# Expert gate's logits with the gate's weights stationary, in four column tiles, and a transposition back

## Chip, cores and metric

The kernel runs on one core of a Trainium2 chip. The metric is the device time of one execution in microseconds; of the kernel before, three timed runs are shown, and one more execution was profiled. Engines: PE is TensorE (PEld its weight loads), DVE VectorE, ACT ScalarE, POOL GpSimd, SP SyncE, which issues most transfers.

## What is computed

One transformer block in float32 over 8 batches of 512 tokens with 256 features: attention with 16 heads and a decayed outer-product memory, a layer norm, a mixture of 8 experts (and two null experts) of which each token takes two, and a second layer norm. Cut to what matters here:

```python
x = _layernorm(x + attention(x))
gate_logits = x @ gate_w.T + gate_b            # 4096 x 256 by 256 x 10
gate_probs = softmax(gate_logits)
weights, selected = top_k(gate_probs, 2)       # null experts get weight 0, the rest is renormalised
combine_w = ...                                # 4096 x 8
out = einsum('te,teh->th', combine_w, einsum('td,edh->teh', x, expert_w) + expert_b)
x = _layernorm(x + out)
```

The change concerns the second line, the gate's logits.

## The kernel before

**Attention turns.** The frame of the program is a loop over 32 units (a batch and a group of four heads), each of eight turns. A turn issues, in this order: `products` (line 182), which computes score blocks twice, once for the running maximum (`mx`, line 192) and once for the exponentials (`sc`, line 196); in some turns projections of later units (`pq` line 165, `pv` line 175), the turned maxima (`pt`, line 233) or the values product (`po`, line 248); then `fill` (line 813), which adds other work. `mx` and `sc` have one PSUM buffer each. So the next turn's `mx` can start when VectorE has taken the maxima of the last (L206, L214) and ScalarE its copy of the diagonal (L210); GpSimd masks that copy (L211) and VectorE reduces it a turn later (L217). In the last turn of a unit the mask is added on TensorE (L205) and VectorE reduces the whole block (L206). A turn is named below by its `mx` block: `mx_2_1`, `mx_1_0`, `mx_1_1` (the last of a unit's cycle), `mx_0_0`.

**Planner.** All other work is written as generators which `fill` and `filled` advance while the program is built. Each turn adds a credit, from what TensorE is thought to have free. A generator yields what its step costs (`yield 0.9`), or `STEP` (go on in the next turn), or `POOL` (GpSimd is wanted, once a turn), or a condition. Generators in `chains` go first, then those in `bulk` (expert tiles, memory sums) as long as credit is left. What stays free in a turn is filled by warming matmuls (`idle`, line 811) that compute nothing that is used. So a step's stated cost decides which expert tile lands in which turn, and the order of every engine's instructions follows from it; this order is kept as written (`in_this_order`). Each engine works through its own list in order.

**The chain of one batch.** `prepare` (line 584) loads x (L596) and adds the output bias to it on GpSimd (L599), later the memory's share (L604, L605) and the inverted denominators (`recs`, L610, L616). `front` (line 636) does the output projection (`pa`), the first norm, eight transpositions of the normed tokens (`px`, L668; copied by ScalarE to `x1T`, L669), the gate's logits (`pg`, L674) and the chain of small VectorE operations on 128 partitions x 40 elements that takes the two best experts: `lg` (L683, adds the gate's bias), maximum, exponent, twice the choice of the largest (L696 to L709), then the weights (L712 to L728). `all_experts` (line 732) turns the weights (`pc`, L740: four matmuls of 32 columns each side by side, copied by ScalarE to `cT`), computes expert tiles (`pex`, L749), adds them with the token's weight on VectorE (L753), adds the bias (`pbias`, L761), and norms (L622 to L628) and stores (`out_y`, L770).

**The gate.** For each of four tiles of 128 tokens the tile of `x1T` is the stationary operand and the gate's weights `gws` (256 x 10, two halves of 128 rows) are the moving one: eight matmuls a batch, in the trace 16 passes, because each float32 matmul shows as two. The logits come out with the tokens on the partitions, 10 columns for each tile, and VectorE reads them from PSUM.

**The end.** The denominators of a batch's softmax go from the last `po` through DRAM: ScalarE's copy (`raw`, L257), store `den` (L258), load `rec` (L267), reciprocal on VectorE (L269), store `dr` (L271), two loads `recs`, GpSimd's product (L616), then `pa`. All these transfers, the loads of x and the stores `out_y` are issued by SP, in its order. PSUM banks other than those of `mx`, `sc` and `po` come from a ring of three (`bank`, line 87).

The lines of the kernel that the diff touches follow.

Of the kernel before, what the change touches and what calls it, by code (L numbers as in the profile page):

```python
# [10 lines left out]
F32 = mybir.dt.float32  # L11
BF16 = mybir.dt.bfloat16
AF = mybir.ActivationFunctionType
ALU = mybir.AluOpType
AX = mybir.AxisListType

P = 128
B, T, D, H, DH = 8, 512, 256, 16, 16
NT = T // P
KC = D // P  # L20
NG = 4
NE, NTRUE = 10, 8
# [12 lines left out]
STEP, POOL = "goes on at the next turn", "needs GpSimd"  # L35
# [22 lines left out]
def bc(ap, axis, n):  # L58

    ap = ap.unsqueeze(axis)  # L60
    shape = list(ap.shape)
    shape[axis] = n
    return ap.to_broadcast(shape)
# [13 lines left out]
def block_kernel(ctx, tc, x, xT, wqk, bqk, wtok, wod, memv, memvb, row, gw, we, eb, out):  # L77
    nc = tc.nc
    PS = bass.MemoryType.PSUM
    const = ctx.enter_context(tc.tile_pool(name="const", bufs=1))  # L80
# [6 lines left out]
    def bank(name):  # L87
        return psB.tile([P, 512], F32, tag="bank", name=name)
# [5 lines left out]
    def load_xT(b):  # L94
        nc.sync.dma_start(xt[:, b], xT[b].rearrange("(k p) t -> p k t", p=P))
# [10 lines left out]
    def vec(n):  # L106
        return rows[:, ROW[n][0] : ROW[n][1]]
# [13 lines left out]
        nc.sync.dma_start(wq[:, :, w, 1], wq_v[:, :, w, 1])  # L121
    for b in range(1, B):
        load_xT(b)
    gws = const.tile([P, KC, NE], F32, name="gws")
    nc.sync.dma_start(gws, gw.rearrange("(k p) e -> p k e", p=P))

    ident = const.tile([P, P], F32, name="ident")
    make_identity(nc, ident)
# [490 lines left out]
    def root(mv, nm):  # L619

        rs = ffp[0].tile([P, NT], F32, tag="rs", name=f"rs_{nm}")
        nc.vector.tensor_scalar(rs, mv[:, :, 1], EPS, None, ALU.add)  # L622
        rr = ffp[0].tile([P, NT], F32, tag="rr", name=f"rr_{nm}")
        nc.gpsimd.tensor_tensor(rr, rs, half, ALU.pow)  # L624
        return rr

    def norm(out_t, in_t, mv, rr, c):
        nc.vector.tensor_scalar(out_t[:, c, :], in_t[:, c, :], mv[:, c, 0:1], rr[:, c : c + 1],  # L628
                                ALU.subtract, ALU.mult)

    def stats(mv, in_t, c, nm):
        bs = ffp[0].tile([P, 6], F32, tag="bs", name=f"bs_{nm}_{c}")
        nc.vector.bn_stats(bs, in_t[:, c, :])
        nc.vector.bn_aggr(mv[:, c, :], bs)

    def front(b):

        yield lambda: b in prepared
        ff, osb, xb = ffp[0], st[b]["osb"], st[b]["xb"]
        y = xb  # L640
        mv = ff.tile([P, NT, 2], F32, tag="mv", name=f"mv1_{b}")
        for c in range(NT):
            pa = bank(f"pa{b}_{c}")
            for k in range(KC):
                nc.tensor.matmul(pa[:, D:], xt[:, b, k, c * P : (c + 1) * P], wt[:, k, CM : CM + D],  # L645
                                 start=(k == 0), stop=(k == KC - 1))
            for k in range(KC):
                nc.tensor.matmul(pa[:, :D], osb[:, k, c * P : (c + 1) * P], wo[:, k, :],  # L648
                                 start=(k == 0), stop=(k == KC - 1))
            nc.vector.scalar_tensor_tensor(y[:, c, :], pa[:, D:], gated[:, c, b : b + 1], xb[:, c, :],  # L650
                                           ALU.mult, ALU.add)
            nc.vector.tensor_tensor(y[:, c, :], y[:, c, :], pa[:, :D], ALU.add)
            stats(mv, y, c, f"a{b}")
            yield 1.9
        yield STEP
        x1 = y
        rr = root(mv, f"a{b}")
        yield STEP
        yield STEP
        for c in range(NT):  # L660
            norm(x1, y, mv, rr, c)
        yield STEP
        yield lambda: b < left[0] + 2
        x1T = ff.tile([P, KC, T], F32, tag="x1T", name=f"x1T_{b}")
        for k in range(KC):
            pt = bank(f"px{b}_{k}")
            for c in range(NT):
                nc.tensor.transpose(pt[:, c * P : (c + 1) * P], x1[:, c, k * P : (k + 1) * P], ident)  # L668
            nc.scalar.copy(x1T[:, k, :], pt)  # L669
            yield 0.7  # L670
        pg = bank(f"pg{b}")
        for c in range(NT):
            for k in range(KC):
                nc.tensor.matmul(pg[:, c * NE : (c + 1) * NE], x1T[:, k, c * P : (c + 1) * P], gws[:, k, :],  # L674
                                 start=(k == 0), stop=(k == KC - 1))
            if c == 1:
                yield 0.9

        def small(n, *shape):
            return ff.tile([P, NT, *shape], F32, tag=n, name=f"{n}_{b}", bufs=1)  # L680

        lg = small("lg", NE)
        nc.vector.tensor_tensor(lg, pg[:, : NT * NE].rearrange("p (c e) -> p c e", e=NE), bc(vec("gb"), 1, NT), ALU.add)  # L683
        yield 0.9
        m1 = small("m1")
        nc.vector.tensor_reduce(m1, lg, AX.X, ALU.max)

        ex = small("ex", NE)
        nc.vector.tensor_tensor(ex, lg, bc(m1, 2, NE), ALU.subtract)
        nc.scalar.activation(ex, ex, AF.Exp)  # L690
        fb = bc(first, 1, NT)
        hot, top = [], m1
        for r in range(2):

            eq = small("eq", NE)
            nc.vector.tensor_tensor(eq, lg, bc(top, 2, NE), ALU.is_equal)  # L696
            nc.vector.tensor_tensor(eq, eq, fb, ALU.mult)
            cd = small(f"cd{r}")
            nc.vector.tensor_reduce(cd, eq, AX.X, ALU.max)
            oh = small(f"oh{r}", NE)  # L700
            nc.vector.tensor_tensor(oh, fb, bc(cd, 2, NE), ALU.is_equal)
            hot.append(oh)
            if r == 0:
                l2 = small("l2", NE)
                nc.vector.scalar_tensor_tensor(l2.rearrange("p c e -> p (c e)"), oh.rearrange("p c e -> p (c e)"), -3.0e38,
                                               lg.rearrange("p c e -> p (c e)"), ALU.mult, ALU.add)
                lg = l2
                top = small("m2")
                nc.vector.tensor_reduce(top, l2, AX.X, ALU.max)  # L709
            yield STEP  # L710
        es = small("es")
        nc.vector.tensor_reduce(es, ex, AX.X, ALU.add)  # L712
        nc.vector.reciprocal(es, es)
        nc.vector.tensor_tensor(ex, ex, bc(es, 2, NE), ALU.mult)
        exf = ex.rearrange("p c e -> p (c e)")
        nc.vector.scalar_tensor_tensor(exf, exf, TINY, exf, ALU.is_ge, ALU.mult)
        w = small("lg", NE)
        nc.vector.tensor_tensor(w, hot[0], hot[1], ALU.add)
        nc.vector.tensor_tensor(w, w, ex, ALU.mult)
        yield STEP  # L720
        dn = small("dn")
        nc.vector.tensor_reduce(dn, w[:, :, :NTRUE], AX.X, ALU.add)
        nc.vector.scalar_tensor_tensor(dn, dn, 0.0, dn, ALU.is_equal, ALU.add)
        nc.vector.reciprocal(dn, dn)
        cwf = ff.tile([P, NT * NTRUE + 32 - NTRUE], F32, tag="cw", name=f"cw_{b}")
        nc.vector.memset(cwf[:, NT * NTRUE :], 0.0)
        cw = cwf[:, : NT * NTRUE].rearrange("p (c e) -> p c e", e=NTRUE)
        nc.vector.tensor_tensor(cw, w[:, :, :NTRUE], bc(dn, 2, NTRUE), ALU.mult)  # L728
        st[b].update(x1=x1, x1T=x1T, cw=cw, cwf=cwf)
        ready.add(b)  # L730
# [45 lines left out]
    def fronts():  # L776
        for b in range(B):
            yield from front(b)
# [78 lines left out]
    for u in range(-1, U + 1):  # L857
        b, g = UNITS[u] if 0 <= u < U else (0 if u < 0 else B, -1)
# [96 lines left out]
```

## Time and profile before

| | us |
|---|---|
| median of 3 runs | 934.79 (931.99 to 935.59) |
| profiled execution, its own time | 936.77 |
| its span | 935.1 |
| mean granted TensorE clock | 0.975 |
| gate: TensorE matmuls L674 (128 passes) | 15.7 busy |
| gate: weight loads L674 (128) | 15.5 busy |
| `lg`, L683 (8) | 1.6 busy |

The span runs from the first to the last instruction; the profiled execution's own time has 1.67 us around it. Busy times of TensorE are modelled at their ends and overlap between neighbouring passes, so the time that a group takes from others is better read from the starts of what stands before and behind it. Attention ends at about 816 us; what follows is mostly expert tiles of batches 5, 6 and 7.

### The profile page before, as it was taken

Reading aid. Unit: us, or ns where it says so; the run is one execution under the profiler, and the core shown is the slowest. Engines: PE = TensorE matmul, PEld = TensorE weight load, DVE = VectorE, ACT = ScalarE, POOL = GpSimd, SP = SyncE. Lnnn points to the kernel's source line nnn. Section 1 sums busy time; section 2 is a strip of 40 time slices with the busy share of each in tenths; the row PEclk is TensorE's granted clock in tenths of the full one; section 3 lists DMA queues with packets and bytes.
Section 4 is the critical chain, followed back from the end, with each engine's and each line's share of the span. In section 5 each row is a group of like instructions: output and inputs, shape, how many; then the busy total and the mean of one; then the engine's idle time right before and its main releaser. Section 6 shows DMA issues by size and latency. Waiting matters only on the chain.

```text
span 935.1 us, 14524 instructions
## 1 busy us (share of the span) xinstructions
PE 868.9 (93%) x5254; PEld 423.1 (45%) x5254; DVE 629.8 (67%) x1449; ACT 344.3 (37%) x746; POOL 376.4 (40%) x682
## 2 busy tenths in 40 slices
PE   8899978798889999999899999999999999999996
PEld 5545544454355544344444344434443344354442
DVE  1344688986876868766778568656765677486765
ACT  4265634344334353444344444343344332200000
POOL 1177785426476645522524345224532352110000
PEclk9999999999899999999989999999999999999998
DMA  7300000000010100000100010001000010010000
GB/s 255 99 13 17 8 7 5 2 2 3 27 46 14 35 27 24 1 2 28 46 1 2 5 55 15 1 3 41 31 2 2 27 47 1 2 48 1 22 23 23
DMA packets 25512, 23.73 MB, mean 25 GB/s; under 512 B 8348, under 2 KB 21180, under 8 KB 25440
## 3 DMA queue, kind: packets, MB, share of 16 engines
q1 hardware_dynamic: 24336, 22.24, 7.5%
q8 instruction: 41, 0.67, 0.3%
q0 software_dynamic: 48, 0.16, 0.2%
q10 hardware_dynamic: 1056, 0.40, 0.2%
q14 instruction: 31, 0.25, 0.1%
HBM read 16.75 MB, written 4.73 MB: 23 GB/s over the span
## 4 chain that ended last, share of the span: by engine, by line
PE 64%; DVE 22%; DMA 4%; POOL 4%; issue 3%; ACT 2%; POOLq 0%; SPq 0%; DVEq 0%; ACTq 0%
PE pex L749 21%; PE mx L192 14%; PE po L248 6%; PE pq L165 5%; DVE negdia L206 3%; DVE x L753 3%; PE pl L349 3%; PE pv L175 2%; PE pa L645 2%; DVE negmax L214 2%; PE pa L648 2%; PE sc L196 2%; PE mx L205 2%; DVE pr L520 1%; DVE ou L518 1%
## 5 line engine op out<-in xcount | busy, mean ns | idle before, releaser
L192 PE MATMUL mx<-qk,qk 32*128 32x128 f32 (+3 forms) x1024 | 219.4, 487 | 39.2 <-DVE negdia L206 27.1
L749 PE MATMUL pex<-ws,x1T 128*128 128x512 f32 x512 | 245.3, 614 | 4.1 <-DVE x L753 3.7
L224 ACT ACTIVATE pe<-sc 128x1024 f32<-128x1024 f32 (+3 forms) x256 | 181.6, 709 | 134.8 <-PE sc L196 122.9
L196 PE MATMUL sc<-qk,qk 32*128 32x512 f32 (+3 forms) x1024 | 211.2, 485 | 1.7 <-ACT pe L224 1.0
L753 DVE SCALAR_TENSOR_TENSOR x<-pex,cw,x 128x256 f32<-128x256 f32 x256 | 123.6, 483 | 101.7 <-PE pex L749 96.5
L226 POOL TENSOR_SCALAR_AFFINE_SELECT pe<-pe 128x256 f32<-128x256 f32 x256 | 105.9, 413 | 165.6 <-ACT pe L224 162.1
L192 PEld LDWEIGHTS mx<-qk,qk 32*128 32x128 f32 x1024 | 84.9, 186 | 154.5 <-DVE negdia L206 47.9
L749 PEld LDWEIGHTS pex<-ws,x1T 128*128 128x128 f32 x512 | 92.1, 192 | 114.0 <-issue 96.6
L206 DVE TENSOR_REDUCE negdia<-mx 128x2 f32<-128x512 f32 (+3 forms) x116 | 92.4, 797 | 73.5 <-PE mx L205 73.4
L211 POOL TENSOR_SCALAR_AFFINE_SELECT dia<-dia 128x256 f32<-128x256 f32 x140 | 57.7, 412 | 185.1 <-ACT dia L210 185.1
L210 ACT COPY dia<-mx 128x256 f32<-128x256 f32 x140 | 52.1, 372 | 212.5 <-PE sc L196 200.1
L214 DVE TENSOR_REDUCE negmax<-mx 128x2 f32<-128x768 f32 (+2 forms) x100 | 73.8, 738 | 44.8 <-ACT dia L210 44.2
L248 PE MATMUL po<-pe,v_aug 128*32 128x512 f32 (+3 forms) x1024 | 98.0, 455 | 0.4 <-POOL pe L226 0.4
L196 PEld LDWEIGHTS sc<-qk,qk 32*128 32x128 f32 x1024 | 79.8, 186 | 10.6 <-issue 5.3
L165 PE MATMUL pq<-xt,wq 128*128 128x512 f32 x128 | 66.1, 642 | 1.1 <-DMA xt<-in_xT 1.1
L217 DVE TENSOR_REDUCE negdia<-dia 128x2 f32<-128x256 f32 x140 | 57.6, 412 | 7.2 <-POOL dia L211 7.2
L169 ACT ACTIVATE qk<-pq,bq 128x512 f32<-128x512 f32 x64 | 46.4, 775 | 25.1 <-PE pq L165 25.1
L624 POOL TENSOR_TENSOR rr_b<-rs_b,half 128x4 f32<-128x4 f32 x8 | 8.1, 1010 | 102.1 <-DVE rs_b L622 102.0
L510 PE MATMUL pm<-ou,dm 128*128 128x144 f32 x256 | 47.6, 317 | 0.9 <-DVE pr L520 0.9
L510 PEld LDWEIGHTS pm<-ou,dm 128*128 128x128 f32 x256 | 37.3, 201 | 19.6 <-issue 16.9
L481 POOL TENSOR_TENSOR ou<-jw,jf 128x288 f32<-128x288 f32 x64 | 44.6, 701 | 1.6 <-PE pm L510 0.4
L248 PEld LDWEIGHTS po<-pe,v_aug 128*32 128x32 f32 x1024 | 20.3, 109 | 38.4 <-issue 19.0
(171 smaller groups left out, 1048.0 us busy)
## 6 DMA issues: line engine op xcount, KB each, us to landing
xt<-in_xT SPq DMA_DIRECT2D x8, 512.0 KB
x<-in_x SPq DMA_DIRECT2D x8, 512.0 KB
recs<-dr SPq DMA_DIRECT2D x16, 256.0 KB
out_y<-x SPq DMA_DIRECT2D x32, 128.0 KB
ws<-in_we SPq DMA_DIRECT2D x2, 1024.0 KB
s<-w SPq DMA_DIRECT2D x8, 127.0 KB
qk<-nt ACTq DMA_DIRECT2D x32, 8.0 KB
wq<-in_wqk SPq DMA_DIRECT2D x3, 128.0 KB
```

The source lines that it names most:

```text
L165: nc.tensor.matmul(pq, wq[:, k, w, g // 2, :], xt[:, b, k, :], start=(k == 0), stop=(k == KC - 1))
L192: nc.tensor.matmul(mx[:, h, :n], qk[m, 0][r, n - P : n], qk[m, 1][r, :n], start=True, stop=m >= BYPASS and (i, pr) != LAST)
L196: nc.tensor.matmul(sc[:, h, :n], qk[v, 1][r, j * P : (j + 1) * P], qk[v, 0][r, j * P :], start=True, stop=True)
L206: nc.vector.tensor_reduce(least, mx[:, :, :n], AX.X, ALU.max, negate=True)
L211: nc.gpsimd.affine_select(out=dia, in_=dia, compare_op=ALU.is_ge, fill=MASKED, base=0, pattern=[[0, 2], [-1, P]], channel_multiplier=1)
L214: nc.vector.tensor_reduce(most, mx[:, :, : n - P], AX.X, ALU.max, negate=True)
L224: nc.scalar.activation(pe[:, :, :n], sc[:, :, :n], AF.Exp, scale=DH**-0.5)
L226: nc.gpsimd.affine_select(out=pe[:, :, :P], in_=pe[:, :, :P], compare_op=ALU.is_ge, fill=0.0, base=0, pattern=[[0, 2], [1, P]], channel_mu ...
L248: nc.tensor.matmul(pos[u][32 * h : 32 * h + 32, j * P :], v_aug[b % 2][:, j, 4 * (g // 2) + h, g % 2 : g % 2 + 2].rearrange("p q d -> p (q ...
L510: nc.tensor.matmul(pm[:, i * HALF * 36 : (i + 1) * HALF * 36], dms[h + i], ou[:, i], start=True, stop=True)
L749: nc.tensor.matmul(pe, x1T[:, k, c * P : (c + 1) * P], ws[:, k, 2 * ep : 2 * ep + 2, :].rearrange("p e h -> p (e h)"), start=(k == 0), sto ...
L753: nc.vector.scalar_tensor_tensor(x1[:, c, :], pe[:, e * D : (e + 1) * D], cw[:, c, 2 * ep + e : 2 * ep + e + 1], x1[:, c, :], ALU.mult, AL ...
```

## The change

The gate's weights become the stationary operand. `gws` is widened from 10 to 32 columns, zeroed by GpSimd before the load, and the load fills the first 10. Each of four column tiles of the array holds a copy of 32 columns; the four tiles of tokens are the moving operand, one for each column tile, and the logits come out as 4 x 32 rows by 128 tokens in one bank. ScalarE copies them to a new tile `lT`, and one transposition by TensorE, in the next turn, brings them back to tokens on partitions, into another bank (`pl`), from which VectorE reads 10 of each 32 columns. The stated costs change from 0.9 in the middle of the eight matmuls and 0.9 after `lg` to 0.6 and `STEP` after the copy and 0.3 after `lg`.

```diff
-    gws = const.tile([P, KC, NE], F32, name="gws")
-    nc.sync.dma_start(gws, gw.rearrange("(k p) e -> p k e", p=P))
+    gws = const.tile([P, KC, 32], F32, name="gws")
+    nc.gpsimd.memset(gws, 0.0)
+    nc.sync.dma_start(gws[:, :, :NE], gw.rearrange("(k p) e -> p k e", p=P))
...
+
         pg = bank(f"pg{b}")
-        for c in range(NT):
-            for k in range(KC):
-                nc.tensor.matmul(pg[:, c * NE : (c + 1) * NE], x1T[:, k, c * P : (c + 1) * P], gws[:, k, :],
+        for k in range(KC):
+            for c in range(NT):
+                nc.tensor.matmul(pg[32 * c : 32 * c + 32, :P], gws[:, k, :], x1T[:, k, c * P : (c + 1) * P],
                                  start=(k == 0), stop=(k == KC - 1))
-            if c == 1:
-                yield 0.9
+        lT = ff.tile([P, P], F32, tag="lT", name=f"lT_{b}", bufs=1)
+        nc.scalar.copy(lT, pg[:, :P])
+        yield 0.6
+        yield STEP
+        pg = bank(f"pl{b}")
+        nc.tensor.transpose(pg[:, :P], lT, ident)
 
         def small(n, *shape):
             return ff.tile([P, NT, *shape], F32, tag=n, name=f"{n}_{b}", bufs=1)
 
         lg = small("lg", NE)
-        nc.vector.tensor_tensor(lg, pg[:, : NT * NE].rearrange("p (c e) -> p c e", e=NE), bc(vec("gb"), 1, NT), ALU.add)
-        yield 0.9
+        nc.vector.tensor_tensor(lg, pg[:, :P].rearrange("p (c e) -> p c e", e=32)[:, :, :NE], bc(vec("gb"), 1, NT), ALU.add)
+        yield 0.3
```

The changed program's instruction order, engine by engine, differs from the old one from the first gate on, because the stated costs move the planner's choices: other turns get the memory sums, expert tiles and warming matmuls.

## The prediction

> **What bounds the kernel now.** I read the page's busy shares and the shares of the chain that ended last, then the windows by stage, then the timelines around single gates.
>
> ```profile
> PE 868.9 (93%) x5254; PEld 423.1 (45%) x5254; DVE 629.8 (67%) x1449; ACT 344.3 (37%) x746; POOL 376.4 (40%) x682
> ...
> PE 64%; DVE 22%; DMA 4%; POOL 4%; issue 3%; ACT 2%; POOLq 0%; SPq 0%; DVEq 0%; ACTq 0%
> ```
>
> TensorE is the main bound, but 22% of the chain lies on VectorE. The windows (span; busy us and count of PE, PEld, DVE, ACT, POOL; clock; DMA) say where:
>
> ```profile
> 300.00:816.44 516.44, 497.35 (x3088) 228.33 (x3087) 354.94 (x876) 209.73 (x432) 208.09 (x408) 0.98 0.06 19
> 816.44:829.69 13.25, 11.68 (x55) 6.74 (x55) 11.31 (x40) 2.17 (x5) 3.62 (x3) 1.00 0.28 85
> 829.69:926.87 97.18, 93.01 (x270) 43.64 (x270) 67.71 (x181) 1.84 (x5) 3.02 (x3) 1.00 0.03 11
> ```
>
> The gates of batches 0 to 5 lie in the first stretch, where attention turns, filled up with other work, follow each other; the gate of batch 6 lies in the second, that of batch 7 in the third. The first and third are TensorE's. The second is a chain of transfers, as the chain of waits in order of time shows (start, us, what):
>
> ```profile
> 816.09 0.40 PE po L248 x8
> 816.51 0.59 ACT raw L257
> 817.12 1.65 DMA den<-raw
> 818.78 1.59 DMA rec<-den
> 820.39 0.56 DVE rec L269
> 820.98 1.43 DMA dr<-rec
> ...
> 823.19 5.05 DMA recs<-dr
> ...
> 828.31 1.34 POOL osb L616
> ```
>
> After the last values product the kernel must bring the last denominators through DRAM, 13.2 us to 829.69; TensorE work in between only covers it. The first stretch has stalls of its own; the largest is at the gate of batch 2 (timeline):
>
> ```profile
> 462.21 1.27 POOL L599 TENSOR_TENSOR x<-x,ob 128x512 f32<-128x512 f32 x1
> ...
> 462.47 1.06 DVE L689 TENSOR_TENSOR ex<-lg,m 128x40 f32<-128x40 f32 x1
> ...
> 464.85 1.74 DVE L705 SCALAR_TENSOR_TENSOR l<-oh,lg 128x40 f32<-128x40 f32 x1
> ...
> 467.65 0.68 DVE L206 TENSOR_REDUCE negdia<-mx 128x2 f32<-128x512 f32 x1
> ...
> 468.38 0.58 PE L192 MATMUL mx<-qk,qk 32*128 32x128 f32 x1 [4.14 <-DVE negdia L206]
> ```
>
> The gate's small VectorE operations stand before the reduction that frees the score bank; beside GpSimd's long operations they take 1.06 and 1.74 us, where undisturbed ones take 0.20; TensorE waits 4.1 us, and the next turn is another 2.0 longer than its like (4.46 against 2.36).
>
> **The gate on TensorE.** Before, one batch's logits are 16 passes (8 matmuls, two passes each):
>
> ```profile
> 862.01 0.43 PE L740 MATMUL pc<-ident,cw 128*32 128x128 f32 x8 [0.24 <-ACT x1T L669]
> 862.37 1.98 PE L749 MATMUL pex<-ws,x1T 128*128 128x512 f32 x4
> ...
> 864.19 1.85 PE L674 MATMUL pg<-gws,x1T 128*128 128x10 f32 x16
> ```
>
> At 0.107 us a pass they hold the engine 1.7 us: the turn with a gate from 559.97 to 562.50 lasts 2.53 us, the turn of the same shape with a pair of expert matmuls (four passes of 0.43) 2.56. After, there are 16 passes of pc's form (32 stationary columns, 128 moving). pc shows 8 in 0.36 us until the next work starts, so four tiles do stream side by side. What eight more cost: po's eight passes of 256 columns keep the next work 0.57 us away, those of 128 columns 0.36, so a second round of 128 columns is 0.21. The new gate: 0.57 us. The transposition is one more instruction; four px take 0.42 us, so 0.11 to 0.13. Saved: 1.7 - 0.57 - 0.13 = 1.0 us a batch. Six gates lie before the last po: -6.0. Batch 6's lies under the denominators' 13.2 us: 0. In the tail (batches 6 and 7) the transposition stands directly behind the gate and waits for the copy: gate's last pass 0.64 after its start, 0.12 to ScalarE (as pc's end to cT, 862.44 to 862.56), the 128x128 copy 0.27, 0.05 back, 0.13: 1.2 against 1.75, so -0.55 for batch 7.
>
> The row holds the changes of array shape around pc. [...] Were each of two such changes a gate to cost a whole pass's latency (0.273) beyond pc's row, six gates would give back 3.3 us and the sum would end near 932.8; by the row nothing is added, and in batches 3 to 5 the new gate follows po, which has its shape.
>
> **What the planner does with it.** The gate now asks for 0.9 us instead of 1.8, and the freed credit moves work. By the changed program's order one more pair of expert matmuls (1.72 us) stands before the last po: +1.7; idle warming matmuls before it fall from 87 to 82 at 0.21 each: -1.1. The pair buys nothing in the tail, because it leaves the 13.2 us, which it doesn't bound.
>
> **VectorE's chain, moved.** In batches 3 to 5 the chain lg to m2 (ten small operations, 1.93 us undisturbed at 866.23) stood behind the reduction L206 and its successors; now it stands before it, the place it had in batch 2. Everything from the norm to the gate comes one turn earlier, and x's add of ob (L599, 1.27 us, twice) falls on it, since x lands 7.8 us after the turn of px begins (554.83 to 562.67). Laid out from that row: px turn 4.4 us, gate turn 2.75, next 2.7; the mask of the diagonal ends at 9.5, the chain at about 13 with one lock, two expert accumulations to 14, L206 to 14.7, where TensorE is through at 13.4: about 1.8 us of stall with the transposition pt. Before, the same turns lost 0, 1.65 and 0.86 in batches 3, 4, 5 (2.36, 3.56+1.65 and 3.22 long). So +2.9, less half of the 4.3 us that the later turns lost to the same chain when it came late (turns from 569.45, 667.65 and 764.37): +0.8. Bounds: -6.8 (all of it gone) to +15.8 (each batch as batch 2 was: 3 x 6.1 - 2.5).
> Batch 2: the chain now meets one L599 and not L544, but the memory gate's operations stand among it (the sums end some six turns earlier). Adding VectorE's operations turn by turn, L206 ends 4.0 us after TensorE, 4.5 with pt, against 6.1: -1.6 (bounds -6.1 to +3). Batches 0 and 1: chain and stalls change places, 0 (within 1.5).
>
> **Queues.** ScalarE's copy (0.27, x8) waits for the gate with nothing behind it but the next turn's copies, which need the next products: 0. The memset of gws goes ahead of ident on GpSimd (0.2 us), under the first transfer that pq waits for; the load of gws waits for it behind 15 larger loads: 0; uncovered 0.2. But at the end SP's queue changes: the last batch's dr now stands behind four stores of out_y, which wait for the norm, and VectorE's reciprocal behind the four norms. From the last po's start: rr_b ends at 3.3, norms at 4.7, reciprocal at 5.25 (before: 4.9); four issues of 0.48 from 3.75 end at 5.6, so dr goes at 5.6 instead of 4.96: +0.65, and its transfer queues behind 512 KB (256 KB of recs take 2.0 us, 826.32 to 828.31). I take +1.5, bounds +0.65 to +3.5. Nothing covers it: TensorE then stands still.
>
> **Sum.** -6.0 - 0.55 + 1.7 - 1.1 + 0.8 - 1.6 + 1.5 = -5.25 us. The profiled execution took 936.77 (span 935.1, the rest around it unchanged), which becomes 931.5; it lies 2.0 above the median of 934.79, so in medians 929.5.
>
> **Rivals.** (1) Off the path: turns that lose TensorE work wait for VectorE instead (67% busy over the span). For it: the stalls above, the 87 idle matmuls; against it: most turns of the first stretch go on without a gap. With half of the six gates' gain (+3.0) it is 932.5, within 0.5%. (2) Slower: the chain in front of L206 meets GpSimd's locks in batches 3 to 5 as in batch 2. At 6.1 us each: 929.5 + 15.0 = 944.5; it decides from about 4.4 us a batch on (3 x 4.4 - 2.5 - 0.8 = 9.9, over the forecast). For it: the place and L599's hour; against it: a pair of expert matmuls now lies in the turn that would wait, which batch 2 did not have. (3) The tiles don't stream side by side: 16 passes at 0.1 as before plus the transposition; -5.25 + 6.0 + 0.8 = +1.5, 936.3. pc's row speaks against it.
>
> **Chances.** Forecast 0.45 (own range 925 to 930.1), rival 1 and smaller mixtures 0.35, rival 2 0.17, rival 3 0.03. What a measurement here can tell is 0.5%, 4.7 us: faster 0.45, same 0.38, slower 0.17. The range takes in the bounds of the stalls at both ends except the worst: 922 to 938.
>
> **What would show it.** Right: 16 passes of pg in about 0.65 us; pl directly behind products in the turns of batches 3 to 5, L206 late by 1 to 2 us there; the last po some 6 to 7 us earlier; from it to the first wait-bound pa 14 to 16 us instead of 13.2. Wrong: pg over 1 us; stalls of 4 us and more before L192 in batches 3 to 5; recs landing as early as before.

## The result, and the profile after

The changed kernel is slower: median 939.55 us (12 runs, 935.73 to 943.74) against 933.58 us for the kernel before in the same session, a ratio of 1.0055 with a 95% interval of 1.0037 to 1.0072. A second session gave 1.006 (1.0035 to 1.0086). Some 5 us were lost where 5 were to be gained.

The profiled execution of the changed kernel, at 935.73 us and a granted clock of 0.985, is the fastest of its twelve, and that of the kernel before (936.77, clock 0.975) one of the slower ones. So the two traces are not to be compared by their totals. Over all its runs each kernel has about the same mean clock (0.977 to 0.978 before; 0.980 and 0.978 after). Busy time and the chain's shares, from the page:

```profile
PE 853.1 (91%) x5258; PEld 409.1 (44%) x5258; DVE 629.4 (67%) x1449; ACT 345.8 (37%) x754; POOL 376.1 (40%) x683
...
PE 55%; DVE 25%; POOL 7%; issue 5%; DMA 4%; ACT 4%; POOLq 0%; SPq 0%; DVEq 0%; ACTq 0%
```

TensorE is busy for 15.8 us less, in part because less of this execution ran at half clock, and its share of the chain fell from 64% to 55%; VectorE's and GpSimd's rose. The windows by the same three stages (columns as before):

```profile
299.12:813.81 514.69, 485.63 (x3088) 217.93 (x3087) 354.17 (x878) 210.88 (x438) 207.39 (x408) 1.00 0.06 19
813.81:827.35 13.54, 9.91 (x59) 5.27 (x58) 11.87 (x41) 2.33 (x6) 3.92 (x3) 0.98 0.25 83
827.35:925.50 98.15, 93.23 (x270) 43.23 (x271) 67.17 (x177) 2.11 (x6) 3.02 (x3) 0.99 0.03 11
```

The attention stretch lost 11.7 us of TensorE's busy time and only 1.75 us of its length: the idle time grew from 19.1 to 29.1 us. Even the 1.75 goes with the clock. In the trace of before TensorE's clock was at half rate for 17 us of the stretch, here for 3.4 (two more executions of each program have 17 and 17, and 3.4 and 6.8, although the mean clocks over all runs are alike). With each turn taken as the mean over those of three executions of its kernel (two of them from the experiments below) in which no half-clock stretch touches it, the stretch takes 509.3 us before and 514.6 after. TensorE's waits in that stretch name what took the rest (us in total, times, longest); `negdia` holds VectorE's maxima that take in the diagonal of a score block (those of L206, L207 after, reduce the whole block), `negmax` those of the columns ahead of it. After:

```profile
PE mx L193 <- DVE negdia L207: 13.1, 8, 3.2
PE mx L193 <- DVE negmax L215: 8.8, 19, 1.3
```

And before:

```profile
PE mx L192 <- DVE negmax L214: 9.5, 21, 1.6
PE mx L192 <- DVE negdia L206: 5.4, 3, 4.1
```

Three waits for the diagonal's reduction (L206 before, L207 after) have become eight. One of them, at the gate of batch 5 (timeline of the changed kernel):

```profile
749.65 0.62 PE L676 MATMUL pg<-x1T,gws 128*32 128x128 f32 x16
...
750.34 0.27 ACT L679 COPY lT<-pg 128x128 f32<-128x128 f32 x1 [0.36 <-PE pg L676]
...
750.85 0.33 PE L683 MATMUL pl<-ident,lT 128*128 128x128 f32 x1
...
751.98 1.26 POOL L600 TENSOR_TENSOR x<-x,ob 128x512 f32<-128x512 f32 x1 [6.03 <-DVE negmax L215]
...
753.20 0.41 POOL L212 TENSOR_SCALAR_AFFINE_SELECT dia<-dia 128x256 f32<-128x256 f32 x1
...
753.63 0.42 DVE L218 TENSOR_REDUCE negdia<-dia 128x2 f32<-128x256 f32 x1 [1.84 <-POOL dia L212]
753.93 1.27 POOL L600 TENSOR_TENSOR x<-x,ob 128x512 f32<-128x512 f32 x1
753.97 0.19 DVE L689 TENSOR_TENSOR lg<-pl,rows 128x40 f32<-128x40 f32 x1
...
754.42 0.84 DVE L695 TENSOR_TENSOR ex<-lg,m 128x40 f32<-128x40 f32 x1
...
756.59 0.77 DVE L711 SCALAR_TENSOR_TENSOR l<-oh,lg 128x40 f32<-128x40 f32 x1
...
758.42 0.68 DVE L207 TENSOR_REDUCE negdia<-mx 128x2 f32<-128x512 f32 x1
...
759.16 0.37 PE L193 MATMUL mx<-qk,qk 32*128 32x128 f32 x1 [2.38 <-DVE negdia L207]
```

The gate itself does what it says: 16 passes in 0.62 us, a copy of 0.27, one transposition. But the logits lie ready in `pl` from 751.2 and `lg` starts at 753.97, because VectorE's queue waits for GpSimd: L218 stands in front of `lg` and waits for the masked diagonal (L212), which GpSimd takes up only after its first addition of `ob` (L600). The chain then runs beside GpSimd's long operations (`ex` 0.84, `l` 0.77, as against 0.20) in front of L207, and TensorE stands still for 2.38 us.

### The profile page after: what moved, and what is told of

The parts are those of the page before. It is cut to its first block, busy times and chain, and to the rows that moved or that the text cites. A ratio compares the mean times of both kernels' runs of the same rounds, so it can differ in the third digit from the quotient of the medians.

```text
span 934.0 us, 14542 instructions
## 1 busy us (share of the span) xinstructions
PE 853.1 (91%) x5258; PEld 409.1 (44%) x5258; DVE 629.4 (67%) x1449; ACT 345.8 (37%) x754; POOL 376.1 (40%) x683
## 4 chain that ended last, share of the span: by engine, by line
PE 55%; DVE 25%; POOL 7%; issue 5%; DMA 4%; ACT 4%; POOLq 0%; SPq 0%; DVEq 0%; ACTq 0%
PE pex L755 20%; PE mx L193 12%; PE po L249 5%; PE pq L166 5%; DVE x L759 4%; DVE negdia L207 3%; PE pa L646 3%; DVE negmax L215 2%; PE pa L649 2%; PE sc L197 2%; DMA s<-w 2%; PE pv L176 2%; DVE pr L521 2%; DVE ou L519 2%; PE pl L350 1%
## 5 line engine op out<-in xcount | busy, mean ns | idle before, releaser
L755 PE MATMUL pex<-ws,x1T 128*128 128x512 f32 x512 | 240.3, 605 | 5.4 <-DVE x L759 3.7
L207 DVE TENSOR_REDUCE negdia<-mx 128x2 f32<-128x512 f32 (+3 forms) x116 | 92.3, 796 | 69.4 <-PE mx L206 69.3
L212 POOL TENSOR_SCALAR_AFFINE_SELECT dia<-dia 128x256 f32<-128x256 f32 x140 | 57.9, 414 | 192.9 <-ACT dia L211 192.7
L215 DVE TENSOR_REDUCE negmax<-mx 128x2 f32<-128x768 f32 (+2 forms) x100 | 73.9, 739 | 53.3 <-ACT dia L211 52.8
L218 DVE TENSOR_REDUCE negdia<-dia 128x2 f32<-128x256 f32 x140 | 57.5, 410 | 9.1 <-POOL dia L212 9.0
L646 PE MATMUL pa<-wt,xt 128*128 128x256 f32 x128 | 36.6, 411 | 1.9 <-DVE x L759 1.9
```

Of the source, the lines that this page charges most:

```text
L207: nc.vector.tensor_reduce(least, mx[:, :, :n], AX.X, ALU.max, negate=True)
L215: nc.vector.tensor_reduce(most, mx[:, :, : n - P], AX.X, ALU.max, negate=True)
L755: nc.tensor.matmul(pe, x1T[:, k, c * P : (c + 1) * P], ws[:, k, 2 * ep : 2 * ep + 2, :].rearrange("p e h -> p (e h)"), start=(k == 0), sto ...
```

## Experiments

Three theories stood at the start. **Schedule**: the new stated costs put the chain in front of the reduction, and its waits eat what TensorE saved. **Off the path**: turns that lose TensorE work wait for VectorE anyway, so the form is worth little wherever it stands. **Clock**: less TensorE work brings more stretches at half clock. Ratios are to the kernel before in the same session; line numbers shift by a few with each edit. Turns are counted from 0 to 255; a turn begins with its first `mx` matmul.

**Form and order apart.** Two kernels swap the parts of the change. The first keeps the old matmuls in the new order:

```diff
+        for c in range(NT):
+            for k in range(KC):
+                nc.tensor.matmul(pg[:, c * NE : (c + 1) * NE], x1T[:, k, c * P : (c + 1) * P], gws[:, k, :],
+                                 start=(k == 0), stop=(k == KC - 1))
         yield 0.6
         yield STEP
...
         yield 0.3
```

> The matmuls of the kernel before (16 passes of pg at 0.107 us, no transposition) stand in the changed kernel's order of work. Schedule theory (the new order makes TensorE wait at L206/L207 in batches 2 to 5, and the cheaper gate hides part of it): slower than the changed kernel by the 6 us that the gate's form was worth where TensorE is the bound, so 1.010 to 1.013 of before. Off-path theory (the saved 1.0 us a batch lies in turns that wait for VectorE anyway): as the changed kernel, 1.004 to 1.007. Clock theory (less TensorE work means more half-rate windows): TensorE has its work back, so 0.998 to 1.003. All: turns with a gate in batches 2 to 5 wait for the diagonal's L206/L207 as they do in the changed kernel if the order is to blame.

Measured: 1.0065 (1.004 to 1.0089), mean clock 0.973. The order alone, with the old form, costs 6 us. Its TensorE work is otherwise that of the changed kernel turn by turn, so that the form can be read from single turns (us, the two traces; the 16 passes of pg stand in turns 181, 213 and 245, the wait for L206/L207 ends turns 183, 215 and 247):

```
turn    old form   new form     turn    old form   new form     turn    old form   new form
181       3.74       2.29       213       3.74       2.29       245       3.74       2.29
182       2.56       2.62       214       2.56       2.62       246       2.56       2.62
183       4.64       6.05       215       4.90       6.38       247       4.95       6.33
184       2.53       2.52       216       2.52       2.53       248       2.53       2.52
```

The gate's turn is 1.45 us shorter, the transposition adds 0.06, and two turns on all of it is given back: VectorE sets the time at which that turn ends.

The second keeps the old order and has the new form; both stated costs are 0.9 again and the turn's end between copy and transposition is gone:

```diff
-        yield 0.6
-        yield STEP
+        yield 0.9
...
-        yield 0.3
+        yield 0.9
```

> The new matmuls and the transposition, with the costs stated as before, so that the order of the rest is that of the kernel before. The transposition stands directly behind the gate and makes TensorE wait for ScalarE's copy, about 0.5 us in batches 2 to 5. Schedule theory: 1.7 - 0.57 - 0.13 - 0.5 = 0.5 saved in four batches and 1.0 in two, less nothing: 0.994 to 0.998 of before. Off-path theory: 0.999 to 1.002. Clock theory: slower than before, 1.003 to 1.006, like the changed kernel, with more half-rate windows in the trace. It decides whether the form or the order makes the changed kernel slower.

Measured: 1.0035 (1.0014 to 1.0055), mean clock 0.981. It is slower than before though nothing is reordered, and its clock is higher, so the clock theory as first stated falls. The gate's turns are 0.42 us shorter, as expected; waits for L215 (12.2 us against 9.5) and L222 (3.2 against 1.1) give it back. What is left over the kernel before was found in turns long ahead of any gate; see the addresses below.

**The chain behind the reduction.** One more turn's end after `lg`:

```diff
         yield 0.3
+        yield STEP
         m1 = small("m1")
```

> The changed kernel with one more turn's end between the logits' bias add and the chain from m1 on, so that in batches 2 to 5 the chain stands behind the diagonal's L206 and not in front of it. Schedule theory: the waits for the diagonal (13.1 us over the turns in the changed kernel) fall to about the 5.4 of before, 5 to 8 us off the changed kernel: 0.997 to 1.000 of before. Off-path theory in its strict form (turns wait for VectorE's total, not for its order): 1.004 to 1.007. Clock theory: 1.004 to 1.007 as well, with as many half-rate windows as in the changed kernel.

Measured: 0.9955 (0.9932 to 0.9978), 9 us under the changed kernel; the waits for negdia fell to 2.5 us. This is what the schedule theory asked for, and somewhat more. A variant that delays the transposition and `lg` as well, by stating 0.9 and 0.9 and keeping the turn's end between them, was expected to be the fastest:

> The new matmuls with the costs stated as before (0.9 and 0.9) and the turn's end between gate and transposition kept: the transposition stands a turn later and waits for nothing, the chain lies behind L206 in batches 3 to 5, and the end has the order of the kernel before (dr ahead of the stores of out_y). Schedule theory: 4 to 6 us off before, 0.993 to 0.997, the fastest of all. Off-path theory: 0.999 to 1.002. Clock theory: 1.003 to 1.006.

Measured: 1.0059 (1.0037 to 1.008). A miss: the waits went to other places in the same stretch (negdia 8.4 us with one of 5.0 in batch 2, negmax 12.3, L222 4.1).

**Addresses.** In every kernel with the wide `gws` three turns before the first gate (10, 18 and 34) were about 0.8 us longer where no half-clock stretch touched them, each on a transfer qk<-nt (the turned maxima, written into the operands of the next scores) that goes out while s<-w does, copies between two buffers of the memory's products (in turn 10 of the kernel before it is issued at 39.06 us, the s<-w ahead of it from 35.01 to 41.41). These come in pairs: 508 pieces of 256 bytes, then three more, whose issue stands behind the 508. The wider tile had moved every tile allocated after it by 160 bytes. One unused tile moves them on by 32:

```diff
     gws = const.tile([P, KC, 32], F32, name="gws")
+    shift = const.tile([P, 8], F32, name="shift")
+    nc.gpsimd.memset(shift, 0.0)
     nc.gpsimd.memset(gws, 0.0)
```

> The changed kernel with one unused tile of 32 bytes a partition behind gws. The wider gws moves every tile allocated after it by 160 bytes, from a multiple of 64 bytes to 32 past one; the unused tile moves them back to a multiple of 64. Address theory: in the traces of all kernels with the wide gws, the eight line-buffer transfers s<-w take 0.5 us longer to issue (6.95 against 6.45 us, mean packet of 256 bytes 19.5 against 18.1 ns) and TensorE's turns 10, 18 and 34 wait 0.84, 0.82 and 0.76 us longer for qk<-nt that goes with them; here these waits are as before and the time falls by 2.4 us, from 1.0055 of before to 1.003. Rival (the lateness comes from the order of work or from chance): the three turns stay late and the time stays at 1.0055.

> The kernel before with the same unused tile of 32 bytes, which moves its tiles off the multiple of 64. Address theory: turns 10, 18 and 34 wait 0.8 us longer each, 1.0025 of before. Rival: no change, 1.000.

Measured: 1.0033 (1.0008 to 1.0059) for the changed kernel, with turns 10, 18 and 34 at 6.03, 3.81 and 3.12 us (before 5.78, 3.81 and 3.12; in the changed kernel 18 and 34 take 4.63 and 3.89). But 0.9992 (0.9973 to 1.0011) for the kernel before, shifted by the same 32 bytes: no loss. So it isn't the multiple of 64. A last kernel moved the tiles of the kernel before by 160 bytes, to the addresses that they have in the changed one:

> The kernel before with an unused tile of 160 bytes a partition behind gws: every later tile has the address that it has in the changed kernel. Address theory (the address itself counts, not the 32 bytes past a multiple of 64, which cost nothing in before_shifted): s<-w takes 7.1 instead of 6.5 us to issue, turns 10, 18 and 34 are 0.8 us longer each, 1.0025 of before. Rival (the wide gws's own transfer or memset delays something): issues of 6.5 us, 1.000.

Measured: 1.0034 (1.0013 to 1.0055), with turns 18 and 34 at 4.61 and 3.87. The issue of the second s<-w of each pair (count; minimum, median and maximum in ns; the first takes 0.73 us in all three kernels) in the kernel before,

```profile
L358 SPq DMA_DIRECT2D s<-w x8: 6399/6474/6577, 35.0 to 119.6; - x8
```

in the changed kernel,

```profile
L359 SPq DMA_DIRECT2D s<-w x8: 6906/7006/7618, 31.2 to 120.3; - x8
```

and in the kernel before at the changed kernel's addresses:

```profile
L360 SPq DMA_DIRECT2D s<-w x8: 6914/7002/7617, 31.1 to 121.6; - x8
```

Addresses alone, with the same program but for an unused tile, cost 2 to 3 us.

**What the form is worth.** The version with the later chain, at good addresses, and the old form in that same order:

> The kernel with the chain behind the diagonal's reduction (0.9955 of before), with the tiles back on a multiple of 64 bytes. Address theory: another 2.4 us off, 0.993 of before. Rival: 0.9955.

> The matmuls of the kernel before (and its narrow gws) in the order of work of the kernel with the chain behind the reduction; beside chain_later_aligned it differs by the gate's form alone. On-path theory (once the chain no longer stands in front of L206, TensorE sets the pace and the form is worth its 1.0 us in each of six batches): 6 us over chain_later_aligned, 0.999 to 1.000 of before. Off-path theory (the turns round the gate wait for VectorE in any order, so the form is worth 0 to 2 us): 0.993 to 0.995, and the whole gain of the later chain is one of order.

Measured: 0.9926 (0.990 to 0.9953) and 1.0021 (0.9999 to 1.0043). The first beats both kernels by 7 us and more. The second fits neither theory: 9 us apart where 6 was the most expected, at a mean clock of 0.973 against 0.980. In turns that no half-clock stretch touches the two traces differ by 2.7 us in all of the attention stretch, which suggested the clock theory turned round: more TensorE work, a lower granted clock. To put back TensorE's time alone, five idle matmuls went in front of each gate:

```diff
         pg = bank(f"pg{b}")
+        for _ in range(5):
+            nc.tensor.matmul(pg[:, 2 * P : 3 * P], ident, ident, start=True, stop=True)
```

> chain_later_aligned with five idle matmuls of 128 columns (1.05 us) in front of each gate's own, which gives TensorE back the time that the form saves and leaves the order alone. Off-path theory in its strict form: the time stays at 0.9926 of before. On-path theory: 6 us over it, 0.999. Clock theory turned round (turns at full clock stay as they are but for some 2 us, and more TensorE work means a lower granted clock): the mean clock falls from 0.980 to about 0.974, as in old_form_chain_later (0.973), and the time is 0.996 to 1.001; in turns without a half-rate window the gate's turn is 1.05 us longer and the next two give most of it back.

Measured: 0.9956 (0.9932 to 0.9979) at a mean clock of 0.981. The turned clock theory falls too, since the clock did not drop. Of the 2.8 us that it is slower, hardly any lie in the attention stretch. The window of that stretch without the idle matmuls,

```profile
299.98:810.88 510.90, 486.41 (x3076) 217.64 (x3075) 355.77 (x878) 210.87 (x438) 207.72 (x408) 0.99 0.06 19
```

and with them:

```profile
295.38:805.76 510.38, 491.75 (x3136) 223.81 (x3135) 352.60 (x878) 211.27 (x438) 207.86 (x408) 0.99 0.06 19
```

TensorE is busy for 5.3 us more in the same time; in turns that no half-clock stretch touches the two differ by 0.8 us. (The gate's turn is 1.45 us longer in batches 2 to 5, and the waits in the turns after it are shorter by 1.4 in batch 2, 1.1 in batch 3, and 0.2 in batch 4, the only one that pays.) What the traces show of the idle matmuls' cost is at the end: from pg of batch 7 to the bias 7.72 us and not 6.49, and half as much in batch 6.

**The changed kernel once more.**

> The changed kernel once more, for a profile that is not its fastest execution and a second ratio. All theories: 1.004 to 1.007 of before; s<-w 7.1 us to issue; L206/L207 waits of 12 to 14 us before the last po. Clock theory as first stated (less TensorE work, more half-rate windows): a mean clock below that of before (0.977). Turned round: at or above it.

Measured: 1.006 (1.0035 to 1.0086), clock 0.978, waits for negdia 13.1 us in 8 places: the same waits to a tenth.

**Which batches.** The later chain by batch, in the changed kernel at good addresses (1.0033):

```diff
         yield 0.3
+        if b in (3, 4, 5):
+            yield STEP
```

> after_aligned with the chain put behind the diagonal's reduction in batches 3, 4 and 5 alone; nine turns' work differs. If these three batches are where the prediction erred (it put their stalls at a net 0.8 us; the traces show some 2 us of TensorE's idle time a batch more than before), the time falls by 4 to 8 us, from 1.0033 to 0.995 to 0.999 of before, and the waits for negdia in them go. If batches 0 to 2 are to blame instead, it stays within 2 us of after_aligned, 1.001 to 1.0035.

The others have `b == 2` and `b in (0, 1, 2)`.

> after_aligned with the chain behind the reduction in batch 2 alone; seven turns' work differs. The prediction had batch 2 gain 1.6 us from the change. If its stall of 3.2 us is the price of the chain's place there, the time falls by 2 to 4 us, to 0.999 to 1.001 of before; if that wait only moves, it stays at 1.003.

> after_aligned with the chain a turn later in batches 0, 1 and 2; 57 turns' work differs, since the planner refills batches 0 and 1. What it takes off beyond later_2 belongs to batches 0 and 1, where the prediction expected no change and TensorE idles 4.3 us more than before: 0.995 to 0.998 of before if half of the 10 us between after_aligned and chain_later_aligned lies here, 1.001 to 1.003 if all of it lies in batches 3 to 5.

Measured: 0.9977 (0.9951 to 1.0003), 1.0013 (0.9989 to 1.0037) and 0.9992 (0.9965 to 1.0019), that is 5.2, 1.9 and 3.8 us under 1.0033. Batches 3 to 5 and 0 to 2 add up to 9.0; all together, in chain_later_aligned, gave 10. Each single difference has some 3 us of uncertainty. TensorE's waits from 540 us to 800, batches 3 to 5, in the changed kernel:

```profile
PE mx L193 <- DVE negdia L207: 8.4, 5, 2.4
PE mx L193 <- DVE negmax L215: 2.4, 7, 0.5
```

With the chain behind the reduction in these batches:

```profile
PE mx L195 <- DVE negmax L217: 5.9, 11, 1.8
PE mx L195 <- DVE negdia L209: 1.3, 2, 0.6
```

And in the kernel before:

```profile
PE mx L192 <- DVE negmax L214: 4.6, 11, 1.4
PE mx L192 <- DVE negdia L206: 1.3, 2, 0.6
```

Put in front, the chain costs 7.1 us of waits for negdia and spares 3.5 of those for negmax, 3.6 in these two traces.

## Why the prediction was wrong

It said 929.5 (922 to 938), most likely faster; measured was 939.55, and 0.55% slower, which it gave 0.17. Through the kernels that hold one part each the loss adds up, beside the prediction's terms:

| part | predicted, us | measured, us | from |
|---|---|---|---|
| order of work: planner, chain, queues | +1.3 (1.7 - 1.1 + 0.8 - 1.6 + 1.5) | +6.1 | old form in the new order, 1.0065 |
| the form on TensorE | -6.55 (-6.0 - 0.55) | -3.0 | from 1.0065 to 1.0033 |
| addresses behind the wider gws | 0 | +2.1 | from 1.0033 to 1.0055 |
| sum | -5.25 | +5.1 | 1.0055 |

Each difference is uncertain by 2 to 3 us; the interval of the sum is 3.5 to 6.7. Nor are the parts free of the clock: old_form_new_plan ran at 0.973 against 0.978 before, which by the relation of time and clock below (5.4 us for 0.01) is an estimated 2.7 of the 6.1. Three steps failed: the price of the new order (off by 4.8 us, most of it VectorE's chain), the worth of the gate's saved work (3.5), and the addresses, put at nothing (2.1).

**The gate on TensorE: the mechanism right, its worth wrong.** The tiles stream side by side, 16 passes in 0.62 us with the next work 0.55 after their start (0.57 predicted), and the saving per gate is larger than the predicted 1.0, 1.39. The step that failed here is "Six gates lie before the last po: -6.0". It counted as time what was TensorE's work. In the turns it is given back two turns later, and 5.3 us put back into the stretch made it 0 to 0.8 us longer: rival 1, off the path, in its full form and not at half. The prediction held against it that most turns go on without a gap; that is true of the turns, but one wait for VectorE every few turns resets them all. The tail's -0.55 was right: from pg to the bias 7.03 before and 6.49 after. Of the -3.0 in the table the traces show these 0.55 and 0.6 to 1.2 in untouched turns; the rest goes with a higher clock (a source of it is under what stays open) or lies within the uncertainty. Rival 3 is ruled out.

**The chain in batches 3 to 5: mis-sized.** Predicted were 1.8 us of stall each, less the 0, 1.65 and 0.86 of before, less 2.15 for relief of later turns, +0.8 in all. Measured was 5.2 us between the two places of the chain; against the kernel before, the two waits in these batches grew by 4.9 us (8.4 and 2.4, from 1.3 and 4.6). The relief was not overrated (waits for negmax fell by 2.2 against before). The stall was 2.8 us a batch and not 1.8, since `lg` does not start when the logits are there but behind VectorE's reduction of the masked diagonal, which waits for GpSimd; and most of the 2.5 us that were subtracted were no waits for VectorE. The turn at 659.05, taken for 1.65 us of stall, holds expert matmuls of 3.52 us that ran in a stretch at half clock (660.5 to 663.9), and takes 3.56 us instead of 5.21 in before_shifted and before_160; waits for negdia in these batches before were 1.3 us in all. Rival 2's 6.1 us a batch was too much (2.0 of it in a turn at half clock, see batch 2 below); the rival had the same place and the same mechanism, and the sign. What the prediction calls a lock shows in the traces as VectorE's operations being slower beside GpSimd's long ones, 0.84 and 0.77 us as against 0.20, and no run shows more of it.

**Batches 0 to 2: expected 0 and -1.6.** The wait in batch 2 did shrink, from 4.14 to 3.2 us. But the 6.1 us from which the prediction worked were not all stall: the next turn, 2.0 longer than its like, ran in a stretch at half clock (465.9 to 472.8). Nor is the wait the same in every execution: it is 4.2 us in before_160 and 0.8 in before_shifted, where a half-clock stretch came earlier (458.4 to 461.9). Moving the chain behind the reduction still takes 1.9 us off there and another 1.9 in batches 0 and 1. What these two cost over the kernel before wasn't isolated; between the chain's two places lies a price that the prediction did not give.

**Queues: the size near, the cause another.** Predicted was +1.5 at the end, through dr behind the stores. From the last po to the end it took 118.9, 118.9 and 119.5 us in three traces of the old order and 120.0 to 120.5 in three of the new. The transfers in the changed kernel:

```profile
816.15 0.33 SPq L268 DMA_DIRECT2D rec<-den  x1
817.34 1.81 SPq L776 DMA_DIRECT2D out_y<-x  x4
...
819.24 0.40 SPq L272 DMA_DIRECT2D dr<-rec  x1
820.82 1.27 SPq L611 DMA_DIRECT2D recs<-dr  x2
...
824.72 2.58 POOL L617 TENSOR_TENSOR osb<-osb,recs 128x512 f32<-128x512 f32 x2 [7.86 <-DMA recs<-dr]
...
826.04 0.70 PE L649 MATMUL pa<-wo,osb 128*128 128x256 f32 x2 [2.63 <-POOL osb L617]
...
827.35 1.22 PE L649 MATMUL pa<-wo,osb 128*128 128x256 f32 x2 [0.61 <-DVE cw L734]
```

dr goes 0.9 us later, but recs, whose packets no longer run among those of out_y, comes in faster (its packets from 822.24 to 825.45, the last of out_y starting at 820.14; before from 823.87 to 827.92, those of out_y from 824.84 on): the pa that needs the second half of `osb` (at 827.35; the product ends at 827.30) starts 13.97 us after po begins and not 13.67. That is +0.3. The rest comes after it. TensorE now idles 2.63 us where the gate's saved work had covered the wait, and a stretch at half clock follows (window, the granted clock in the third column from the end):

```profile
826.83:830.24 3.41, 2.89 (x7) 2.35 (x8) 2.03 (x5) 0.00 (x0) 0.47 (x1) 0.50 0.00 0
```

It is there in all three traces of the changed order, 12 to 13 us after the last po, and in none of the three of the kernel before (nor in chain_later and chain_later_aligned, which took 119.4 and 118.0 us from the last po to the end); pa ends 1.2 to 1.7 us later, the 0.3 among them.

**The load of gws and its memset at 0.** They cost nothing themselves. The width of the tile did, through the addresses behind it, and nothing in the prediction looked there.

What stays open: why old_form_chain_later and old_form_new_plan were granted a clock of 0.973 where padded_later, with as much TensorE time in the gate, had 0.981 (together with it, 6 us between two kernels that differ only in the gate's form); and which property of an address makes s<-w slow. For the clock the traces hold a lead that none of the theories named. This is the gate of batch 4 in the kernel before, with the 3.4 us that hold it and the next 3.4 (timeline; then windows, the granted clock third from the end):

```profile
657.16 1.95 PE L674 MATMUL pg<-gws,x1T 128*128 128x10 f32 x16
```

```profile
657.09:660.50 3.41, 3.41 (x38) 2.44 (x34) 1.94 (x6) 1.47 (x3) 0.00 (x0) 1.00 0.47 154
660.51:663.92 3.41, 3.41 (x8) 1.18 (x4) 1.76 (x5) 0.00 (x0) 3.25 (x5) 0.50 0.00 0
```

TensorE shows no idle time in the first, and yet the second is at half clock. Of the 20 gates of batches 2 to 5 in the five traces with the old form, seven are followed by such a stretch within 1.7 us, in each case with all 16 passes in the 3.4 us ahead of it; of the 44 in the eleven traces with the new form, none is. So the old form, whose passes move only 10 columns each, seems to cost clock as well as time, which the idle matmuls of 128 columns did not put back. No run tested it by itself, and 13 of the 20 gates, all four in old_form_new_plan's trace among them, show nothing of the kind; the prediction had no term for the clock.

## What to carry to other kernels

An engine that is busy 93% of the time is still not the bound of every turn: before crediting saved work to the end, follow the next two or three turns to the first wait for another engine, and count only what is left behind it. If an edit re-plans the order, price the new place of every chain on the second engine first; here one line that put the chain behind the reduction turned 1.0033 into 0.9926. And a tile that changes its size moves all that is allocated after it (here by 160 bytes, which cost 2 to 3 us): compare the transfers that ran before the edited code is reached.

## What the runs showed of the hardware

The same program with its tiles at other addresses runs SBUF-to-SBUF transfers of 256 bytes at other speeds: 6.5 us (median) to issue the second s<-w of a pair, behind the 508 pieces of the first, with the tiles where they were (the kernel before), and 7.0 at 160 bytes on (the changed kernel and before_160); the slowest quarter of the packets of 256 bytes takes 20 to 28 ns in the changed kernel, where 18 held in the kernel before for all but the slowest twentieth. At 32 bytes on the kernel before lost nothing (0.9992), and at 192 bytes on the turns 18 and 34 of the changed kernel were back at 3.81 and 3.12 us. No run shows why 160 bytes are slower.

TensorE's clock falls to half for stretches of 3.4 us or a multiple (but for the last one, at the execution's end), five to ten times in an execution (ten in the trace of before, seven in that of the changed kernel), and where they fall differs between executions; over half of the variance between executions goes with the mean clock (0.01 of it with 5.4 us, over all kernels, each about its own mean). In these two traces the changes of the clock, the start and the end aside, are a whole number of 3.41 us apart. In the changed kernel it fell at 826.83 after 3.4 us of which TensorE had idled 2.63, and in the kernel before at 660.51 after 3.41 us in which the profile shows no idle time at all, but all 16 passes of an old gate. A turn made longer by such a stretch looks like a stall in a table of turns (4.46 us against 2.36 behind the gate of batch 2 in the kernel before), so the granted clock has to be read beside it.
